# Two graph-attention layers: own queries by rank kept on chip, rank products behind the first query, first loads in the order of their use

## The chip, the cores and the metric

The kernel runs on one core of a Trainium2 chip. The metric is device time in microseconds (us), the median of several runs; smaller is better. The engines are TensorE (PE in the profile, its weight loads PEld), VectorE (DVE), ScalarE (ACT), GpSimd (POOL) and SyncE (SP). SP, ACT and POOL also issue DMA transfers. A line such as L568 is a line of the kernel's file.

## The reference

A graph of N = 2708 nodes has features of width 512. Two layers of the same form are applied, each with its own weights (8 heads of width 64, hidden width 2048):

```python
mask = adj.astype(jnp.float32) + jnp.eye(n, dtype=jnp.float32)
q = (h @ Wq.T + bq).reshape(n, N_HEADS, D_K)
k = (h @ Wk.T + bk).reshape(n, N_HEADS, D_K)
v = (h @ Wv.T + bv).reshape(n, N_HEADS, D_K)
scores = jnp.einsum('nhd,mhd->hnm', q, k) / jnp.sqrt(jnp.float32(D_K))
scores = jnp.where(mask[None, :, :] == 0, jnp.float32(-1000000000.0), scores)
attn = jax.nn.softmax(scores, axis=-1)
ctx = jnp.einsum('hnm,mhd->nhd', attn, v).reshape(n, D_MODEL)
h1 = _layer_norm(h + ctx @ Wo.T + bo, ln1_g, ln1_b)
ff = jax.nn.relu(h1 @ W1.T + b1) @ W2.T + b2
h2 = _layer_norm(h1 + ff, ln2_g, ln2_b)
```

The adjacency is sparse (a node has some nine neighbours with itself), symmetric, given as 2708 x 2708 int32.

## The kernel before, in words

**Lists in place of masks.** `by_edges` turns each row of the adjacency into a list of at most 24 neighbours and then attends only over lists: keys and values are gathered row by row from HBM. A second path, `by_rows`, runs only where a row has too many neighbours; it is not run with these inputs. Nodes are worked on in 22 tiles of 128 (the last, number 21, has 20 nodes). In `first`, tile t means nodes in their given order; everything behind it uses nodes sorted by the length of their list, and tile g then means ranks 128 g to 128 g + 127. `CAPS[g]` is the longest list in tile g, 22 for g = 0 down to 3 for g = 21. The attention goes through the tiles in `order`: 21, 20, then 19, 18, then 8, 9 and so on, two to a block of the feed-forward part.

**Stage 1, `first`.** For each tile, k and v are projected from x (columns of xT, loaded in blocks `xg` of 256 nodes) and written to `kv_d`. At the same time `lists` loads rows of the adjacency (`aj`, two buffers), POOL adds the diagonal (L656), ScalarE squares into `code` (L660), and VectorE takes the greatest eight of each of 11 pieces and merges them (L663 to L670). When all lists are there, `counted` works out the lengths and prefix counts on VectorE (L684 to L732), `ranked` multiplies them with a triangle and with ones on TensorE (L742, L749) to get each node's rank, writes each node's list to its rank in `rec_d` by 22 indirect DMAs (L768), reads all back into `new`, and makes `ident_i`, the node of each rank (L794). `listed` makes `idx` and `minus` of it.

**Stage 2, `first_queries`.** q of all nodes is projected tile by tile in their given order and written to `q_d`, two tiles per DMA (`written`). The attention needs q by rank, and so a gather from `q_d` once all of it is there. To begin earlier, `own_rows` gathers rows of x by rank, `turned_own` transposes them, and `own_query` projects them: at t = 9 (OWN) for tiles 21 and 20, whose q stays on chip in `own`; at t = 11 for tiles 19 and 18, whose q is written to `q_own` in HBM and read back by `asked`. Between these q, `advance` and `through` move the attention on: a generator, `attend`, whose step k multiplies one pair of gathered neighbours with q (`weights`, L991 and L997), weighs the values of the step before (`weigh`, L1010 to L1030), sums the tile that ended two steps before (`sums`) and divides the one that ended three before (`divided`, L1061, making `cx`). `advance` adds to a credit that steps use up; it stops while two finished tiles wait in `got`. `loads` gathers keys and values ahead, into five buffers.

**Stage 3, the blocks.** `attended` transposes cx (L1100), projects with Wo (L568, `o`), adds x by rank and normalises; `turned` transposes the result to `hT`. `feed_forward` runs 16 steps f: pf = W1 times hT (L1265, three PSUM buffers), relu on ScalarE to `ft` (L1273), and, three steps behind, the second product into `a` (L1253). At f = 10 the next block's cx is transposed, at f = 11 its `o` is made, behind f = 15 its `hT`. Keys and values of the next layer are made from each finished block (`keys_values`).

**What sets the order.** On PE, ACT and SP the order of instructions is that of the program text throughout (`manual_schedule`). On POOL this holds in stages 1 and 2, on VectorE in stage 2; elsewhere a scheduler orders these two. A wait at the head of an engine holds whatever is written behind it. So what `advance` writes between two relus stands between them on ScalarE.

Of the kernel before, what the change touches and what calls it, by code (L numbers as in the profile page):

```python
# [18 lines left out]
P = 128  # L19
# [26 lines left out]
OWN = 9  # L46
# [424 lines left out]
def by_edges(ctx: ExitStack, tc: tile.TileContext, x, xT, adj, layers, out, good):  # L471
# [32 lines left out]
    own = {}  # L504
    at = None
# [15 lines left out]
    q_own = dram.tile([N, DM], F32, name="q_own")  # L521
# [280 lines left out]
    def first(w, meanwhile):  # L802
# [20 lines left out]
        load()  # L823
        wk = matrix(w, "Wk", "wk")
        turning = turned_row(cols[1], "bk", 1.0)
# [5 lines left out]
        for t in range(NT):  # L831
            r = size(t)
            xs = tokens(t, 0)
            kv = wts.tile([P, 2 * DM], F32, tag=f"w2_{5 + t % 3}", name="kvs")
            k = project(xs, r, wk, "k")
            if t == 0:
                finish(turning)
            nc.vector.tensor_tensor(kv[:r, :DM], k[:r], bk[:r], ALU.add)
            if t == NT - 1:
                ranked(*counts)  # L840
            v = project(xs, r, wv, "v", other=True)
            nc.scalar.copy(kv[:r, DM:], v[:r])
            if before:
                nc.scalar.dma_start(**before)
            before = dict(out=kv_d[0][t * P : t * P + r, :], in_=kv[:r])
            if t == 0:
                load()
            while done < min(NT, 1 + LEAD * t):
                lists(done)
                done += 1  # L850
                if done == NT:
                    counts = counted()
            meanwhile(t)
            if t == QT:
                wq = matrix(w, "Wq", "wq")
                turning = turned_row(cols[0], "bq", DK**-0.5)
                bq = next(turning)
                finish(turning)
        nc.scalar.dma_start(**before)
        return bq, wq, listed, pa, tokens  # L860

    def first_queries(bq, wq, listed, pa, tokens, meanwhile):

        nonlocal at
        xrs = [own_rows(g) for g in blocks[0]]
# [12 lines left out]
        for t in range(NT):  # L878
# [10 lines left out]
            if t == OWN - 1:  # L889
# [15 lines left out]
        while made:  # L905
            written()

# [11 lines left out]
    def own_query(g, zT, to, bq, wq):  # L919
# [4 lines left out]
        if g in blocks[1]:  # L924
            nc.sync.dma_start(out=q_own[g * P : g * P + r, :], in_=to[:r])
# [183 lines left out]
    class Layer:  # L1109
# [27 lines left out]
        def load_second(self, part, temp):  # L1137
# [3 lines left out]
            def sum_of(one, tag, other):  # L1141
                t, u = row(w, one, tag), temp()
                nc.sync.dma_start(out=u, in_=other.to_broadcast([P, DM]))
                nc.vector.tensor_tensor(t, t, u, ALU.add)
# [200 lines left out]
    def attend(n, got):  # L1345
# [15 lines left out]
        for k, step in enumerate(steps):  # L1361
            if step:
                g, s0, c, i, last = step
                if i == 0:
                    t = Tile(g, q)
# [3 lines left out]
                if i == 1 and g != order[-1]:  # L1369
# [36 lines left out]
    early = {}  # L1406

    def beside_keys(t):
# [3 lines left out]
        if t > NT - 3:  # L1412
            now.load_second(t + 2 - NT, temp)
# [3 lines left out]
    def beside_queries(t):  # L1417

        if len(now.w2) < 5:
            now.load_w1(len(now.w1), nc.scalar)  # L1420
            now.load_w2(len(now.w2), nc.scalar)
        if t > OWN:
            advance(1.0 if t < NT - 7 else 0.45)
        if t == NT - 7:
# [3 lines left out]
        if t == NT - 6:  # L1428
# [10 lines left out]
    for j in range(len(now.w1), NFC // 2):  # L1439
        now.load_w1(j)  # L1440
        now.load_w2(j)
    behind, pool = None, []
    for n in range(NL):
# [26 lines left out]
        turning = projecting = None  # L1470
        for k, block in enumerate(blocks):
# [4 lines left out]
            for f, zs in enumerate(now.feed_forward(block, hs, hT)):  # L1476
# [8 lines left out]
                if more and f == 10:  # L1485
# [29 lines left out]
                if not last and not more:  # L1515
# [7 lines left out]
                    if f == 7:  # L1523
                        finish(ahead)
                        pool += nxt.preloaded(order[:8], temp)
            if not last:
# [79 lines left out]
```

## Time and profile before

| | |
|---|---|
| median of 3 runs | 1984.96 us (1980.67 to 1987.98) |
| profiled execution | 1984.12 us, of which span 1982.0 us |
| TensorE busy | 1903.5 us, 96% of the span; granted clock 0.985 |
| VectorE, ScalarE, POOL busy | 1303.1, 934.6, 798.3 us |
| DMA | 367.96 MB, 186 GB/s over the span |
| stage 1 | to about 172 us; adjacency, x and weights come at about 330 GB/s |
| stage 2 | 172 to 285 us |
| first feed-forward block | 290 to about 357 us |

All times of the trace count from the span's start. In a timeline each line is: start, length, engine, line, operation, written tile <- read tiles, shape, count, and in brackets how long the engine was idle before it and what ended that. A matmul of 128x512 in float32 counts as two records in it. SPq and ACTq are the issuing of DMAs by these engines.

### The profile page before, as it was taken

How to read it: one execution, taken by the hardware profiler on the slowest of the kernel's cores; microseconds unless marked ns; L12 is line 12 of the kernel's file. 1: busy time of each engine (PE TensorE's matmuls, PEld its weight loads, DVE VectorE, ACT ScalarE, POOL GpSimd, SP SyncE). 2: the span in 40 equal slices, each digit the busy share in tenths (PEclk: the TensorE clock that was granted, in tenths of full speed). 3: DMA queues.
4: the chain of work that ended last, by engine and by line, in shares of the span. 5: the costliest groups of instructions: out<-in, count | busy, mean ns of one | idle time of the engine just before them, and what ended most of it. 6: DMA issues, size and time to landing. Idle time of an engine off the chain costs nothing. (4 is left out here: it accounts for less than half of the span.)

```text
span 1982.0 us, 20873 instructions
## 1 busy us (share of the span) xinstructions
PE 1903.5 (96%) x6162; PEld 1104.5 (56%) x6162; DVE 1303.1 (66%) x2140; ACT 934.6 (47%) x3219; POOL 798.3 (40%) x708
## 2 busy tenths in 40 slices
PE   8999888999999999999999997999999999999997
PEld 3443344565656556566566643556666566666664
DVE  6884478675957969568442025888587989777421
ACT  4660235464545646447441112665446765655320
POOL 3104436362634636435210023455356655544210
PEclk9999899999999999999999998999999999999998
DMA  8988658464745747455310746756465766554100
GB/s 321 357 296 293 191 200 296 154 208 143 227 154 174 236 150 246 154 173 176 133 58 22 225 157 225 258 182 212 155 208 186 244 205 225 177 188 151 42 11 13
DMA packets 131518, 367.96 MB, mean 186 GB/s; under 512 B 16701, under 2 KB 36525, under 8 KB 128687
## 3 DMA queue, kind: packets, MB, share of 16 engines
q0 software_dynamic: 69104, 246.35, 37.6%
q1 hardware_dynamic: 55780, 103.86, 15.3%
q10 hardware_dynamic: 6510, 16.34, 2.2%
q8 instruction: 50, 0.82, 0.2%
q14 instruction: 74, 0.60, 0.1%
HBM read 315.14 MB, written 51.35 MB: 185 GB/s over the span
## 5 line engine op out<-in xcount | busy, mean ns | idle before, releaser
L952 POOL DMA_INDIRECT kv<-kv_d,idx x420 | 547.0, 1302 | 494.0 <-DVE acc L1030 337.2
L1253 PE MATMUL a<-w,ft 128*128 128x512 f32 (+1 forms) x1408 | 665.3, 597 | 9.5 <-ACT ft L1273 9.5
L1265 PE MATMUL pf<-hT,w 128*128 128x256 f32 (+1 forms) x2816 | 638.2, 374 | 15.8 <-ACT ft L1273 8.0
L1265 PEld LDWEIGHTS pf<-hT,w 128*128 128x128 f32 x2816 | 523.2, 192 | 193.4 <-issue 107.7
L1253 PEld LDWEIGHTS a<-w,ft 128*128 128x128 f32 (+1 forms) x1408 | 255.9, 186 | 234.1 <-issue 198.3
L1273 ACT ACTIVATE ft<-pf,b 128x256 f32<-128x256 f32 (+1 forms) x352 | 157.9, 458 | 424.4 <-PE pf L1265 424.1
L991 DVE TENSOR_TENSOR kv<-kv,q 128x1024 f32<-128x1024 f32 (+3 forms) x222 | 256.5, 1158 | 144.6 <-DMA kv<-kv_d,idx 122.0
L1017 ACT ACTIVATE kv<-kv,p 128x64 f32<-128x64 f32 x1232 | 311.0, 335 | 5.0
L997 DVE TENSOR_REDUCE sc<-kv 128x16 f32<-128x1024 f32 (+3 forms) x222 | 254.6, 1153 | 1.0
L1030 DVE TENSOR_TENSOR acc<-acc,kv 128x1024 f32<-128x1024 f32 (+2 forms) x178 | 203.8, 1145 | 35.9 <-ACT kv L1017 35.4
L1090 POOL TENSOR_TENSOR rd<-va,mhalf 128x1 f32<-128x1 f32 (+1 forms) x88 | 85.7, 974 | 270.0 <-DVE va L1088 268.6
L1010 ACT ACTIVATE p<-sc,minus 128x8 f32<-128x8 f32 (+1 forms) x420 | 103.3, 295 | 190.3 <-DVE sc L997 189.9
L1023 DVE TENSOR_TENSOR kv<-kv,p 128x512 f32<-128x512 f32 (+1 forms) x178 | 121.5, 683 | 69.5 <-ACT p L1010 69.5
L568 PE MATMUL o<-wo,cT 128*128 128x512 f32 (+1 forms) x352 | 155.1, 593 | 0.5 <-ACT cT L1105 0.5
L568 PEld LDWEIGHTS o<-wo,cT 128*128 128x128 f32 (+1 forms) x352 | 65.1, 186 | 86.5 <-issue 75.8
L1061 ACT ACTIVATE cx<-acc,su 128x64 f32<-128x64 f32 (+1 forms) x352 | 88.5, 333 | 42.4 <-DVE su L1053 34.9
L1285 DVE TENSOR_TENSOR h<-a,h 128x512 f32<-128x512 f32 (+1 forms) x44 | 29.7, 677 | 106.0 <-PE a L1253 105.9
L1094 DVE SCALAR_TENSOR_TENSOR h<-h,rd,ln_b 128x512 f32<-128x512 f32 (+1 forms) x88 | 65.8, 748 | 48.1 <-POOL rd L1090 48.1
L660 ACT ACTIVATE code<-aj 128x2708 bf16<-128x2708 int32 (+1 forms) x22 | 73.3, 3330 | 48.1 <-POOL aj L656 41.2
L663 DVE MAX8 tops<-code 128x8 f32<-128x247 f32 (+2 forms) x242 | 82.8, 400 | 18.6 <-ACT code L660 18.5
L1017 ACT ACTIVATE acc<-kv,p 128x64 f32<-128x64 f32 (+1 forms) x352 | 88.8, 334 | 1.4
L568 PE MATMUL k<-wk,xg 128*128 128x512 f32 (+1 forms) x176 | 82.1, 611 | 6.8 <-DMA wk<-in_Wk 6.7
(132 smaller groups left out, 1466.3 us busy)
## 6 DMA issues: line engine op xcount, KB each, us to landing
aj<-in_adj SPq DMA_DIRECT2D x21, 1354.0 KB, 11.8
w<-in_W SPq DMA_DIRECT2D x26, 512.0 KB, 4.8
kv_d<-kvs ACTq DMA_DIRECT2D x21, 512.0 KB, 7.2
xg<-in_xT SPq DMA_DIRECT2D x20, 512.0 KB, 7.0
kv<-kv_d,idx POOLq DMA_INDIRECT x420, 5.6
q_d<-qs SPq DMA_DIRECT2D x22, 256.0 KB, 4.7
zT_d<-zT SPq DMA_DIRECT2D x22, 256.0 KB, 5.3
xb_d<-h SPq DMA_DIRECT2D x21, 256.0 KB, 5.3
```

The source lines that it names most:

```text
L568: nc.tensor.matmul(o[:r], xs(c), wm[:, c, :], start=(c == 0), stop=(c == NC - 1))
L952: nc.gpsimd.indirect_dma_start(out=to, out_offset=None, in_=table[:, :], in_offset=bass.IndirectOffsetOnAxis(ap=s, axis=0), bounds_check=N ...
L991: nc.vector.tensor_tensor(kv[:r, :c, :DM], kv[:r, :c, :DM], self.q[:r].unsqueeze(1).to_broadcast([r, c, DM]), ALU.mult,)
L997: nc.vector.tensor_reduce(self.sc[:r, s0 : s0 + c, :], kv[:r, :c, :DM].rearrange("p s (h d) -> p s h d", d=DK), AX.X, ALU.add,)
L1010: nc.scalar.activation(p[:r, s, :], self.sc[:r, s, :], AF.Exp, bias=minus[:r, g, s : s + 1])
L1017: nc.scalar.activation(to[:, i, hd], kv[:r, i, DM + h * DK : DM + (h + 1) * DK], AF.Copy, scale=p[:r, s0 + i, h : h + 1],)
L1023: nc.vector.tensor_tensor(to[:, 0, :].rearrange("p (h d) -> p h d", d=DK), kv[:r, 0, DM:].rearrange("p (h d) -> p h d", d=DK), p[:r, s0, : ...
L1030: nc.vector.tensor_tensor(self.acc[:r, :c, :], self.acc[:r, :c, :], kv[:r, :c, DM:], ALU.add)
L1061: nc.scalar.activation(cx[:r, hd], self.acc[:r, 0, hd], AF.Copy, scale=self.su[:r, h : h + 1])
L1253: nc.tensor.matmul(a[:r], fts[f][:, c0 : c0 + r], self.w2[f // 2][:, f % 2, :], start=(f == 0), stop=(f == NFC - 1),)
L1265: nc.tensor.matmul(pf[:, :w], self.w1[f // 2][:, c, f % 2 * P : f % 2 * P + P], hT[:, c, :w], start=(c == 0), stop=(c == NC - 1),)
L1273: nc.scalar.activation(ft[:, :w], pf[:, :w], AF.Relu, bias=self.b1[:, f : f + 1])
```

## The change

1. First loads: the first block of x is loaded in two halves. SP issues the first half, then the first quarter of Wk, bk, the rest of Wk, bq, and then the second half; before, bq and bk came first, then the whole block and Wk.
2. Rank products: `ranked` moves from between k and v of the last key tile to behind the first q of stage 2; the rows of x by rank are gathered right behind it.
3. Own queries: three tiles (21, 20, 19) in place of four. All three are gathered and transposed together at t = 11, and their q stays on chip; `q_own` is gone. Tile 18's q comes from `q_d` like all later ones: `asked` gives None until all q are written, and `attend` then yields None, at which `advance` stops.
4. The attention beside the queries is paced anew: `through(0)` and the first block's transpositions at t = 16 in place of 15, its `o` at t = 17 in place of 16, 0.6 in place of 0.45 credit behind that.
5. The two sums of bias rows with b2 and bo (`load_second`) are made behind q 3 in place of in stage 1.
6. The last three pairs of W1 and W2 pieces are loaded on ACT's queue at f = 0, 2, 4 of the first block, in place of SP's queue before it.
7. In the first block, the next block's transpositions and `o` come at f = 11 and 12 in place of 10 and 11. In layer 0's blocks POOL keeps the order of the program text.

```diff
-OWN = 9
+OWN = 11
@@ first
-            nc.sync.dma_start(out=t[:, :, :bw], in_=chunked(xT)[:, :, b : b + bw])
             xg.append(t)
+            step = bw if i else P
+            for a in range(0, bw, step):
+                nc.sync.dma_start(
+                    out=t[:, :, a : a + step], in_=chunked(xT)[:, :, b + a : b + a + step]
+                )
+                yield
...
-        cols = given_column(w, "bq"), given_column(w, "bk")
-        load()
-        wk = matrix(w, "Wk", "wk")
-        turning = turned_row(cols[1], "bk", 1.0)
+        wk = wts.tile([P, NC, DM], F32, tag="wk", name="wk")
+        halves = load()
+        next(halves)
+        for c in range(NC):
+            nc.sync.dma_start(out=wk[:, c, :], in_=chunked(w["Wk"])[:, c, :])
+            if c == 0:
+                cols = [given_column(w, "bk")]
+        cols.append(given_column(w, "bq"))
+        finish(halves)
+        turning = turned_row(cols[0], "bk", 1.0)
...
-            if t == NT - 1:
-                ranked(*counts)
@@ first_queries
-        xrs = [own_rows(g) for g in blocks[0]]
...
             q = project(tokens(t, 1), r, wq, "q", other=t % 2 > 0)
+            if t == 0:
+                ranked(*counts)
+                xrs = [own_rows(g) for g in order[:3]]
...
-                for g in blocks[0]:
+                for g in order[:3]:
                     own[g] = at.tile([P, DM], F32, tag="q", name="q", bufs=QB)
...
-            if t in (OWN, OWN + 2):
-                k = (t - OWN) // 2
-                zTs = [turned_own(g, xr) for g, xr in zip(blocks[k], xrs)]
-                for g, xr, zT in zip(blocks[k], xrs, zTs):
-                    own_query(g, zT, to.get(g, xr), bq, wq)
+            if t == OWN:
+                zTs = [turned_own(g, xr) for g, xr in zip(order, xrs)]
+                for g, zT in zip(blocks[0], zTs):
+                    own_query(g, zT, to[g], bq, wq)
                     advance(0.5)
-                xrs = [own_rows(g) for g in blocks[1]] if k == 0 else []
+            if t == OWN + 2:
+                own_query(order[2], zTs[2], to[order[2]], bq, wq)
             meanwhile(t)
         while made:
             written()
+        all_made.append(True)
@@ own_query
-        if g in blocks[1]:
-            nc.sync.dma_start(out=q_own[g * P : g * P + r, :], in_=to[:r])
@@ asked
+        if n == 0 and not all_made:
+            return None
         q = at.tile([P, DM], F32, tag="q", name="q", bufs=QB)
-        if n == 0 and g not in blocks[1]:
-            gather(q[:r], q_d[0], ident_i[:r, g : g + 1])
-        else:
-            table = q_own if n == 0 else q_d[n]
-            nc.sync.dma_start(out=q[:r], in_=table[g * P : g * P + r, :])
+        fetch(n, q, q_d[n], g)
@@ attend
                 if i == 0:
-                    t = Tile(g, q)
+                    while q is None:
+                        q = asked(n, g)
+                        if q is None:
+                            yield None
+                    t, q = Tile(g, q), None
...
-                if i == 1 and g != order[-1]:
+                if i > 0 and q is None and g != order[-1]:
@@ beside_keys, beside_queries
-            now.load_second(t + 2 - NT, temp)
+            now.load_second(t + 2 - NT, temp, sums)
...
+        if t == 3:
+            for total, other in sums:
+                nc.vector.tensor_tensor(total, total, other, ALU.add)
...
-            advance(1.0 if t < NT - 7 else 0.45)
-        if t == NT - 7:
+            advance(1.0 if t < NT - 6 else 0.6)
+        if t == NT - 6:
             through(0)
...
-        if t == NT - 6:
+        if t == NT - 5:
@@ by_edges, the blocks
-    for j in range(len(now.w1), NFC // 2):
-        now.load_w1(j)
-        now.load_w2(j)
...
+        in_order = ExitStack()
+        if n == 0:
+            in_order.enter_context(tc.manual_schedule(engines={mybir.EngineType.Pool}))
...
-                if more and f == 10:
+                if more and f == 10 + (k + n == 0):
...
-                if more and f == 11:
+                if more and f == 11 + (k + n == 0):
...
-                advance(PACE[n] if k else 1.1 if f < 10 else 0.4)
+                advance(PACE[n] if k else 1.1 if f < 11 else 0.4)
...
+                if k == 0 and len(now.w1) < NFC // 2 and f % 2 == 0:
+                    now.load_w1(len(now.w1), nc.scalar)
+                    now.load_w2(len(now.w2), nc.scalar)
```

More of the change, by code (lines that the diff above doesn't have):

```diff
@@ L504, in by_edges @@
     own = {}
+    all_made = []
     at = None
@@ L520, in by_edges @@
     q_d = [dram.tile([N, DM], F32, name=f"q_d{n}") for n in range(NL)]
-    q_own = dram.tile([N, DM], F32, name="q_own")
     zT_d = [None] + [dram.tile([NT, P, NC, P], F32, name=f"zT_d{n}") for n in range(1, NL)]
@@ L817, in tokens @@
             if c0 == 0 and len(xg) < 2 * XBS:
-                load()
+                finish(load())
             xs = xg[i + again * XBS]
             return lambda c: xs[:, c, c0 : c0 + size(t)]
-        cols = given_column(w, "bq"), given_column(w, "bk")
-        load()
-        wk = matrix(w, "Wk", "wk")
-        turning = turned_row(cols[1], "bk", 1.0)
+        wk = wts.tile([P, NC, DM], F32, tag="wk", name="wk")
[8 more added lines that the diff above has]
+        turning = turned_row(cols[0], "bk", 1.0)
         bk = next(turning)
@@ L846, in first @@
             if t == 0:
-                load()
+                finish(load())
             while done < min(NT, 1 + LEAD * t):
@@ L855, in first @@
                 wq = matrix(w, "Wq", "wq")
-                turning = turned_row(cols[0], "bq", DK**-0.5)
+                turning = turned_row(cols[1], "bq", DK**-0.5)
                 bq = next(turning)
@@ L859, in first, with first_queries @@
         nc.scalar.dma_start(**before)
-        return bq, wq, listed, pa, tokens
-    def first_queries(bq, wq, listed, pa, tokens, meanwhile):
+        return bq, wq, counts, ranked, listed, pa, tokens
+    def first_queries(bq, wq, counts, ranked, listed, pa, tokens, meanwhile):
         nonlocal at
-        xrs = [own_rows(g) for g in blocks[0]]
         made = []
@@ L1135, in load_w2, with load_second @@
             self.w2.append(t)
-        def load_second(self, part, temp):
+        def load_second(self, part, temp, later=None):
             w = self.w
@@ L1143, in sum_of @@
                 nc.sync.dma_start(out=u, in_=other.to_broadcast([P, DM]))
-                nc.vector.tensor_tensor(t, t, u, ALU.add)
+                if later is None:
+                    nc.vector.tensor_tensor(t, t, u, ALU.add)
+                else:
+                    later.append((t, u))
                 return t
@@ L1405, in by_edges @@
     ahead = attend(0, got)
-    early = {}
+    early, sums = {}, []
     def beside_keys(t):
@@ L1525, in by_edges @@
                         pool += nxt.preloaded(order[:8], temp)
+            in_order.close()
             if not last:
```

## The prediction

> **What bounds the kernel now.** I began with the busy times of the page: TensorE is busy for 96% of the span, so only its idle time and its slow clock can be won, and each matmul taken away counts in full.
>
> ```profile
> PE 1903.5 (96%) x6162; PEld 1104.5 (56%) x6162; DVE 1303.1 (66%) x2140; ACT 934.6 (47%) x3219; POOL 798.3 (40%) x708
> ```
>
> Next I cut the first 360 us, the part that the diff touches, where TensorE stops (busy time by stretch; the columns are the stretch, its length, busy us and instructions of PE, PEld, DVE, ACT and POOL, granted clock, DMA share, GB/s).
>
> ```profile
> 6.72:159.64 152.92, 152.86 (x360) 67.23 (x360) 122.03 (x438) 82.90 (x43) 19.55 (x55) 1.00 0.93 333
> 159.64:172.16 12.52, 8.06 (x17) 3.30 (x17) 8.12 (x27) 0.00 (x0) 1.11 (x1) 0.73 0.68 236
> 206.76:217.69 10.93, 1.59 (x8) 1.21 (x8) 1.41 (x4) 0.23 (x1) 7.10 (x8) 0.66 0.52 152
> 285.16:290.37 5.21, 0.00 (x0) 0.00 (x1) 5.17 (x8) 3.47 (x16) 2.29 (x2) 0.86 0.81 297
> 308.36:323.00 14.64, 7.81 (x24) 4.08 (x25) 14.11 (x18) 8.51 (x33) 9.19 (x8) 0.88 1.01 366
> ```
>
> There are five stalls: the start (6.72 us), the rank matmuls (from 159.64), the rows of x by rank (206.76), the turned rows of the first block (285.16), and the middle of the first feed-forward block (308.36). Each one also lowers the clock after it. The timeline of TensorE shows what each waits for:
>
> ```profile
> 164.10 1.22 PE L742 MATMUL pr<-hot,tri 128*128 128x264 f32 x2 [4.46 <-DVE kvs L838]
> ...
> 213.55 0.58 PE L1100 MATMUL tp<-ident,xr 20*128 20x20 f32 x4 [6.79 <-DMA xr<-in_x,ident_i]
> 216.68 1.09 PE L1100 MATMUL tp<-ident,xr 128*128 128x128 f32 x4 [2.55 <-DMA xr<-in_x,ident_i]
> 217.69 8.66 PE L568 MATMUL q<-wq,zT 128*20 128x512 f32 x16
> ...
> 290.37 6.88 PE L1265 MATMUL pf<-hT,w 128*128 128x148 f32 x32 [5.21 <-ACT hT L1105]
> ...
> 313.20 2.34 PE L1265 MATMUL pf<-hT,w 128*128 128x148 f32 x8 [4.84 <-ACT ft L1273]
> ...
> 319.88 1.27 PE L1265 MATMUL pf<-hT,w 128*128 128x148 f32 x8 [1.99 <-ACT ft L1273]
> ```
>
> The last two are not ScalarE's own slowness. Its relus stand in order behind attention weights, these behind VectorE, and VectorE behind a gather of q (timelines of POOL, DVE and ACT):
>
> ```profile
> 299.71 2.46 POOL L952 DMA_INDIRECT q<-q_d,ident_i  x1 [0.30 <-issue]
> ...
> 307.34 1.22 DVE L991 TENSOR_TENSOR kv<-kv,q 128x1024 f32<-128x1024 f32 x1 [5.93 <-issue]
> ...
> 317.54 2.02 ACT L1061 ACTIVATE cx<-acc,su 128x64 f32<-128x64 f32 x8
> ```
>
> From 350 us on, the waits of TensorE are small (10.6 us up to 1180), and the change leaves that part as it is.
>
> [...] 16 passes of 128x512 take 8.66 us at 217.69, where 32 warm ones at 241.31 take 13.90, so a long stop costs 1.7 us more. A wait of 1.99 us costs nothing here, one of 2.80 (at 1650 us) some 1.8. [...] So a gather from q_d waits for all twelve writes; the trace has it after the last one. [...] the stretch from 308 shows a DMA share of 1.01.
>
> **The change, part by part.** Times are those of the profiled execution (span 1982.0 us, 1984.12 in all; the median is 1984.96, 0.84 above). From the first block's end on, the written order of all engines is unchanged, so the sum ends there.
>
> *First loads.* The first real load is issued at 0.79 in place of 1.72 us, and the first matmul needs 512 KB in place of 768: an estimate of 1.4 us earlier. This does not reach the end whole. The last key tiles wait for VectorE to empty PSUM (0.88 us at 156), and VectorE works through lists that come through two adjacency buffers: 7 us from issue to landing at the end of that stage, 0.5 on POOL, 3.3 on ScalarE, in a loop. Ahead of the first adjacency load lie as many bytes as before, so that loop starts 0.9 us earlier. I take 0.9 (bounds 0 and 1.4). One more issue on SP costs 0.45 us of SP alone, hidden by the transfers.
>
> *Rank matmuls behind the first q.* They wait for VectorE's counting, to 163.9. TensorE now does the last v (3.4) and, once PSUM is free at 163.9, the first q (3.4), then the four rank products warm (1.8), to 169.1; eleven more q at 3.43 end at 206.9. Before, ten q were done at 206.76; now twelve are: +6.9 us. The ranks themselves hardly move: VectorE's wait for a bias row (2.37 us at 168.11) goes, the q ahead of the rank products takes its place: 0.3 us earlier. So **the wait for x by rank stays**, and I count nothing for it. The two bias sums move behind q 3, where VectorE idles 2.7 us a q.
>
> *Three q in one group.* The third transposition waits for a third gather, issued at 211.9 (where the first kv gather was); with the second's 6.1 us it lands at 217.9. The first own q starts at 218.2: -0.5. The kv gathers behind it on POOL start 1.3 us later; their first reader comes at 223.5, so that is covered. The fourth own q (3.43 us) and its transposition (0.5) are gone: +3.9. Two writes and two reads of q_own leave SP, and with them VectorE's wait of 6.85 us at 268.
>
> *Attention beside the q.* Own q end at 226.7, q 12, 13, own 19 and q 14 to 16 at 247.3. Next come the transpositions of cx. VectorE's list up to the sum of tile 20, at 0.6 us per 512 elements, ends at 248.3, ScalarE's cx 2 us later: TensorE waits 2.7 us there (new), and with even odds loses 1.9 of clock: 3.7 together. Then q 17, both o, q 18 to 21 and the transpositions take 25.8: 276.4 after the 0.9 from the start. ScalarE no longer has tile 18's weights ahead of hT, so hT takes 1.4 in place of 5.2 us. Feed-forward begins at **277.7 in place of 290.37**.
>
> *The q of tile 18.* It now comes from q_d, so it waits for the last q. From that q's end on VectorE (276.1), the write takes 3, POOL 1, the gather 4.5 to 5: 285. (Before, 294.88 to 307.34, 12.5 us, with POOL busy and the DMA engines full.) Two steps of attention are written behind the first relu, so relu 1 stands behind tile 18's first weights. From 285: four VectorE passes of 1.13 us, of which three come before the weights (288.5), weights 2.5, two loads issued 1.1, relu: 292.5. TensorE has run out at 284 and waits 8.6 us. Then ScalarE alone sets the pace: four more weights at 2.5, one at 0.3, two cx at 2.0, four load issues (2.2), four relus: relu 5 at 310.7. Before, the same point was 319.9, since only the three steps of tile 8 (12.2 us) stood behind the late q. **Gain at that point: 9.1 us.** The wait of 2.8 us ahead of it costs up to 1.7 of clock: -0.8. Attention's projection one f later leaves h no slack (h was done 3 us before its transposition): -0.5.
>
> *POOL by hand, W loads on ScalarE.* POOL's order behind the first block is the old one: nothing. The last six W loads no longer come in one burst at 295 to 301; they are needed from f = 10 on, some 20 us after issue, and took 8.2 us on that queue.
>
> Sum: 9.1 - 0.8 - 0.5 = 7.8, about **8 us**: 1984.96 - 8 = 1977.
>
> **Rivals.** (1) *Short waits.* cx is ready sooner (no clock loss, 1 us less wait: 3 us), q lands at 283 (2 us), the start brings 1.4: 13 to 15 us, 1971. For it: fewer transfers at 276 to 290 than in the burst before. Against: q can't overtake the last write.
> (2) *Another wait in the same place.* VectorE's order puts the next layer's bias column (L1161 before) ahead of tile 18's products. If this column takes the 15.2 us that its neighbour took, VectorE starts at 292.7 and the gain is about 0: 1985. Against: that was under a full DMA load; other columns took 6.5 to 7.2.
> (3) *Slower.* The block ends 24 us of ScalarE work after q 18 is there. Break-even is q landing at 294, a loss of 10 us at 304, 28 us after the last q. That needs POOL's two kv gathers ahead of the q gather to be held by a buffer that VectorE frees late: 1995. Against: their buffers are free from 262 on.
>
> **How the numbers follow.** About 0.5% (10 us) is what a measurement of this kernel can tell from no change. Forecast 0.56 (4 to 12 us of gain), rival 1 0.26, rival 2 0.12, rival 3 0.06. Faster: rival 1 and the forecast's upper end (0.11), 0.37; slower 0.06; same 0.57. The range from 1967 to 1986 takes in rival 1 and most of rival 2; the forecast's own is 1973 to 1981.
>
> **What would show it.** Right: TensorE's first matmul near 5.3 us; no stop of over 1 us at the rank products; a stop from about 206 to 218; feed-forward from about 278; then a stop of 7 to 9 us behind ScalarE's relu, with VectorE waiting for q. Wrong: no stop at f = 4, feed-forward after 283, or stops beyond 360 us that were not there.

## The result and the profile after

| | before | changed kernel |
|---|---|---|
| median | 1982.49 us (1976.43 to 1987.98, 12 runs) | 1979.45 us (1975.20 to 1986.72, 12 runs) |
| ratio to before | | 0.9981, 95% interval 0.9968 to 0.9994 |
| once more, with the experiments | 1982.02 us (42 runs) | 1978.20 us (21 runs); 0.9977, 0.9970 to 0.9985 |
| profiled execution: span | 1982.0 us | 1978.1 us |

The gain is 3 to 4.5 us. It is clear of noise, since both intervals lie below 1, but it is under the 0.5% of the prediction's cases, and about half of the 8 us forecast or less.

The page's busy times say where a gain can't have come from: TensorE has only 2.4 us less work, the fourth own query and its transposition less what a slower clock adds (granted 0.983 over the span, before 0.985).

```profile
PE 1901.1 (96%) x6150; PEld 1100.9 (56%) x6150; DVE 1300.5 (66%) x2139; ACT 933.6 (47%) x3218; POOL 790.7 (40%) x708
```

The timeline of TensorE in the changed kernel answers to the stops shown of before:

```profile
4.77 5.21 PE L568 MATMUL k<-wk,xg 128*128 128x512 f32 x8 [4.77 <-DMA wk<-in_Wk]
...
161.93 3.70 PE L568 MATMUL q<-wq,xg 128*128 128x512 f32 x8 [0.93 <-DVE kvs L849]
...
211.78 0.58 PE L1108 MATMUL tp<-ident,xr 20*128 20x20 f32 x4 [6.61 <-DMA xr<-in_x,ident_i]
214.61 1.09 PE L1108 MATMUL tp<-ident,xr 128*128 128x128 f32 x4 [2.25 <-DMA xr<-in_x,ident_i]
216.33 1.09 PE L1108 MATMUL tp<-ident,xr 128*128 128x128 f32 x4 [0.63 <-DMA xr<-in_x,ident_i]
217.35 8.29 PE L568 MATMUL q<-wq,zT 128*20 128x512 f32 x16
...
277.66 4.31 PE L1276 MATMUL pf<-hT,w 128*128 128x148 f32 x32 [0.54 <-ACT hT L1113]
...
290.45 2.34 PE L1276 MATMUL pf<-hT,w 128*128 128x148 f32 x8 [6.45 <-ACT ft L1284]
...
307.19 1.36 PE L1276 MATMUL pf<-hT,w 128*128 128x148 f32 x8 [2.43 <-ACT ft L1284]
...
384.32 6.58 PE L568 MATMUL v<-wv,zT 128*128 128x512 f32 x8 [5.56 <-DVE kvs L1327]
```

Read from the top. The start is earlier, the stop of 4.46 us ahead of the rank products has become 0.93 us ahead of the first q, the stop for x by rank is still there, the 5.21 us ahead of the feed-forward part are 0.54, and the stop ahead of f = 4, which waits for the relu of f = 1, is there as expected. (The first relu, of f = 0, is done by 279.4 us. Some texts of the experiments call the one of f = 1 "the first relu".) The last line is the surprise. It lies at 384 us, well behind the first block, in a part that the prediction took as unchanged: the value projection of layer 1's keys and values (`keys_values`) stands still for 5.56 us, and then runs its eight records in 6.58 us in place of some 3.6: the granted clock is 0.56 in this stretch, where it was 1.00 in the projection before the stop. Before, the same matmul waited 0.27 us and took 3.70:

```profile
390.10 3.70 PE L568 MATMUL v<-wv,zT 128*128 128x512 f32 x8 [0.27 <-DVE kvs L1316]
```

Both traces have the same 2816 records of `pf` in the same order. So the start of one and the same record in both timelines, before minus after, is the gain up to that point:

| record of `pf` | before, us | after, us | gain |
|---|---|---|---|
| first (block 1, f = 0) | 290.4 | 277.7 | 12.7 |
| 65th (block 1, f = 8) | 319.9 | 307.2 | 12.7 |
| 129th (block 2, f = 0) | 358.3 | 347.2 | 11.1 |
| 193rd (block 2, f = 8) | 397.1 | 394.2 | 2.9 |
| 257th (block 3, f = 0) | 439.0 | 435.9 | 3.1 |
| last | 1961.5 | 1957.7 | 3.8 |

11.1 us are won by the end of the first block, 8.2 of them are lost between 378 and 391 us, and behind that the number moves by some 2 us (2.9 to 5.1). The question is what the 8.2 us were lost to. This table is used for every experiment below, because it shows where a gain comes and goes, which a median with an interval 3 to 8 us wide can't. But it is one execution of each kernel. A second execution of the changed kernel (the last experiment) has a gain of 12.4 us at the 129th record, 6.4 at the 257th and 8.6 at the end: 1.3, 3.3 and 4.8 more than the first. So places and waits are read from it, and differences of a few us at the end are not.

### The profile page after: what moved, and what is told of

The parts are those of the page before. It is cut to its first block, busy times and chain, and to the rows that moved or that the text cites. A ratio compares the mean times of both kernels' runs of the same rounds, so it can differ in the third digit from the quotient of the medians.

```text
span 1978.1 us, 20841 instructions
## 1 busy us (share of the span) xinstructions
PE 1901.1 (96%) x6150; PEld 1100.9 (56%) x6150; DVE 1300.5 (66%) x2139; ACT 933.6 (47%) x3218; POOL 790.7 (40%) x708
## 5 line engine op out<-in xcount | busy, mean ns | idle before, releaser
L1335 POOL DMA_INDIRECT kv_d<-kvs,ident_i x22 | 23.3, 1060 | 164.2 <-ACT kvs L1329 97.1
```

## The experiments

Each ratio is to the kernel before, run beside it. "Gain" means the table's column, from the experiment's profiled execution.

### Two parts alone: first loads, rank products

The kernel before with part 1 of the change alone:

```diff
-        load()
-        wk = matrix(w, "Wk", "wk")
+        halves = load()
+        next(halves)
+        for c in range(NC):
+            nc.sync.dma_start(out=wk[:, c, :], in_=chunked(w["Wk"])[:, c, :])
...
+        finish(halves)
```

> The kernel before with one part of the change: the first loads in the order of their use, with half of x's first block. The prediction gave this part 1.4 us at the first matmul, of which 0.9 us was to reach the end; the trace of the changed kernel shows 1.95 us at the first matmul and 3.2 us from the second tile on. If TensorE carries it through the first 210 us: 3 us at the end, 1979.5 to 1980.5 us. If the first own query still waits for x by rank, which follows GpSimd's and VectorE's ranks and not TensorE, and the gathers set what follows: 0 to 1 us, 1982 to 1983 us.

1982.24 us; ratio 0.9992 (0.9982 to 1.0002). TensorE starts 1.86 us earlier and carries that unchanged to the last q at 280 us, through the wait for x by rank, so the second theory is wrong on the place, though its time is the one that came. At the start of block 2 0.9 us is left. By the medians this part is worth about 1 us (1983.25 less 1982.24), near what the forecast put down, but its interval takes in no gain at all.

The kernel before with the rank products and the gathers of x behind the first q, and no more:

```diff
-            if t == NT - 1:
-                ranked(*counts)
...
             q = project(tokens(t, 1), r, wq, "q", other=t % 2 > 0)
+            if t == 0:
+                ranked(*counts)
+                xrs = [own_rows(g) for g in blocks[0]]
```

> The kernel before with one part of the change: the rank matmuls and the gathers of x by rank behind the first q, with the first own query still behind the ninth q. TensorE's stop of 6.5 us ahead of the first q goes (the changed kernel shows 8.5 us gained there), but the rows of x by rank come no earlier. If the stop only moves: TensorE waits some 6 to 10 us longer ahead of the first own query, and the time is 1982 to 1984 us. If it is not all paid back there: 1978 to 1981 us.

1983.16 us; ratio 0.9997 (0.9984 to 1.0011): nothing. The timeline of TensorE shows the stop in its new place, 11.55 us where before had 6.79:

```profile
164.95 3.70 PE L568 MATMUL q<-wq,xg 128*128 128x512 f32 x8 [0.93 <-DVE kvs L838]
...
212.88 0.58 PE L1100 MATMUL tp<-ident,xr 20*128 20x20 f32 x4 [11.55 <-DMA xr<-in_x,ident_i]
```

The gain is 5.4 us at the third q and 0.4 us at the own query. Alone the part pays nothing. In the changed kernel OWN = 11 puts two more q into the wait. Parts 3 to 5 of the change were not run alone, so what each brings to the 12.7 us at the first `pf` is not shown.

### The last loads of W1 and W2

The changed kernel with the six last loads on SP in one burst again:

```diff
+    for j in range(len(now.w1), NFC // 2):
+        now.load_w1(j)
+        now.load_w2(j)
...
-                if k == 0 and len(now.w1) < NFC // 2 and f % 2 == 0:
-                    now.load_w1(len(now.w1), nc.scalar)
-                    now.load_w2(len(now.w2), nc.scalar)
```

> The last six loads of W1 and W2 are issued by SyncE in one burst behind the last q again, as in the kernel before; all else as in the changed kernel. The prediction put the burst beside the gather of tile 18's q as a cost of the kernel before, and charged the change 1.1 us of ScalarE for each pair of loads. If the burst is what counts: the q of tile 18 lands 3 to 8 us later than 284.0 us, the first relu at 293 to 298, and the gain at the end of the first block is 4 to 8 us in place of 11.1; 1979 to 1983 us. If ScalarE's issues are what counts: fifth relu up to 4 us earlier, 1975 to 1979 us.

1983.18 us; ratio 1.0003 (0.9993 to 1.0012): without this part the whole change brings nothing. The first theory holds. In the timelines of VectorE the first product with tile 18's q waits for its gather, in the changed kernel and then in this one:

```profile
284.06 2.36 DVE L999 TENSOR_TENSOR kv<-kv,q 128x1024 f32<-128x1024 f32 x2 [0.93 <-DMA q<-q_d,ident_i]
```

```profile
287.70 2.36 DVE L999 TENSOR_TENSOR kv<-kv,q 128x1024 f32<-128x1024 f32 x2 [4.46 <-DMA q<-q_d,ident_i]
```

POOL issues that gather at the same time in both (280.57 and 280.34 us); it lands 3.6 us later beside the burst. The busy times by stretch say why (the last columns are granted clock, DMA share and GB/s), again the changed kernel and then this one:

```profile
280.00:290.00 10.00, 4.00 (x20) 2.17 (x18) 8.04 (x12) 4.19 (x18) 5.44 (x5) 0.89 0.68 200
```

```profile
280.00:290.00 10.00, 4.17 (x22) 2.34 (x20) 4.34 (x7) 1.98 (x8) 4.97 (x5) 0.86 0.98 340
```

A DMA share of 0.98 and 340 GB/s: the DMA engines are full with weights issued at 277.5 to 281.7 us, which nobody needs before f = 10 at 321.5 us. VectorE falls from 8.04 to 4.34 us busy while it waits, TensorE then stops for 9.92 us ahead of f = 4 and 5.05 us ahead of f = 8, and the gain goes from 12.5 us (first record) to 6.8 (65th) and 4.5 (129th). The stop ahead of the values takes the rest (3.99 us of it here).

On the other side of the same edit, the two issues on ScalarE cost it nothing. The timeline of ScalarE in the changed kernel, with ACTq for the issues:

```profile
288.11 0.35 ACT L1025 ACTIVATE acc<-kv,p 128x64 f32<-128x64 f32 x1
288.21 0.37 ACTq L1135 DMA_DIRECT2D w<-in_W  x1
288.36 0.57 ACT L1025 ACTIVATE acc<-kv,p 128x64 f32<-128x64 f32 x2
288.76 0.39 ACTq L1142 DMA_DIRECT2D w<-in_W  x1
288.84 1.29 ACT L1025 ACTIVATE acc<-kv,p 128x64 f32<-128x64 f32 x5
290.03 0.36 ACT L1284 ACTIVATE ft<-pf,b 128x148 f32<-128x148 f32 x1
```

The eight passes run from 288.11 to 290.13, 2.02 us, exactly as long as eight passes with no issue between them (2.02 at 290.81). The relu of f = 1 follows at once. The other two pairs lie among eight passes each too, which take 2.02 us at 295.42 and 2.01 at 304.85.

### POOL's order

The list of the change says that POOL keeps the order of the program in layer 0's blocks. In the code that ends with the first block (`in_order.close()` stands behind its last step), so only this block has it.

Three theories for the lost 8.2 us. (1) POOL in the order of the program sends a gather of keys and values late, and attention falls behind. (2) Taking the contexts at f = 11 and 12 holds attention back. (3) Attention, bound by its gathers, can't follow a TensorE that is 11 us earlier; whatever is done, a stop appears.

POOL free in the first block:

```diff
-            in_order.enter_context(tc.manual_schedule(engines={mybir.EngineType.Pool}))
+            pass
```

> POOL is no longer put in the order of the program in layer 0's blocks; all else as in the changed kernel (about 1979.5 us; the kernel before about 1982.5). Theory 1, POOL's order costs attention its lead: the gather 9.3 goes out ahead of the two short powers again, some 10 us earlier than at 340.6 us, the gathers behind it follow, VectorE adds bk to the keys of layer 1 about 5 us earlier, TensorE's 5.56 us before the values of layer 1 shrink to under 1 us, and the time is 1972 to 1975. Theory 3, attention can't follow TensorE whatever POOL's order: 9.3 may go out earlier, but the stop before the values stays at 4 to 6 us and the time within 1.5 us of 1979.5.

1975.73 us (8 runs); ratio 0.9963 (0.9949 to 0.9978). The gain is 10.6 us at the 65th record, 8.5 at the 129th, 8.9 at the 257th: the stop ahead of the values is gone. The time lies between the ranges of the two theories. The gather called 9.3 brings tile 9's fourth pair of neighbours, in two DMAs. In the timeline of POOL both stand in the changed kernel behind the second of two short powers of the norm (`rd`), which itself waits for VectorE:

```profile
338.82 1.60 POOL L1098 TENSOR_TENSOR rd<-va,mhalf 128x1 f32<-128x1 f32 x1 [2.43 <-DVE va L1096]
340.60 1.52 POOL L962 DMA_INDIRECT kv<-kv_d,idx  x1 [0.19 <-issue]
342.42 1.46 POOL L962 DMA_INDIRECT kv<-kv_d,idx  x1 [0.30 <-DVE kv L999]
```

With POOL free the first of the two stands ahead of both powers and the second between them, each 6.2 us earlier:

```profile
334.35 0.99 POOL L962 DMA_INDIRECT kv<-kv_d,idx  x1 [0.30 <-issue]
335.36 0.65 POOL L1098 TENSOR_TENSOR rd<-va,mhalf 128x1 f32<-128x1 f32 x1
336.19 1.56 POOL L962 DMA_INDIRECT kv<-kv_d,idx  x1 [0.18 <-issue]
```

What hangs on it is seen on VectorE. First the changed kernel, where it waits for that gather at 344 us, for a next one at 365 us, and so comes to the keys of layer 1 at 383.60; then POOL free, where the first of these waits is missing:

```profile
348.33 1.23 DVE L999 TENSOR_TENSOR kv<-kv,q 128x1024 f32<-128x1024 f32 x1 [4.19 <-DMA kv<-kv_d,idx]
...
371.68 1.22 DVE L999 TENSOR_TENSOR kv<-kv,q 128x1024 f32<-128x1024 f32 x1 [6.81 <-DMA kv<-kv_d,idx]
...
383.60 1.27 DVE L1327 TENSOR_TENSOR kvs<-k,bk 20x512 f32<-20x512 f32 x2
```

```profile
367.98 1.22 DVE L999 TENSOR_TENSOR kv<-kv,q 128x1024 f32<-128x1024 f32 x1 [4.64 <-DMA kv<-kv_d,idx]
...
380.64 1.43 DVE L1327 TENSOR_TENSOR kvs<-k,bk 20x512 f32<-20x512 f32 x2
```

L1327 takes k out of PSUM. The four projections of a pair of tiles (k, v, k, v) share a PSUM tag of three buffers, so the fourth can't start before the first k is out. In the kernel before this began at 389.38 us, so VectorE is only 5.8 us earlier in the changed kernel where TensorE was 11.1 us earlier.

But the earlier gather is only a part of why the stop is gone. With POOL free VectorE comes to the keys 3.0 us earlier (380.64 against 383.60), and TensorE comes to the projection before the stop 2.6 us later (377.64 against 375.06). The two together make up the 5.56 us. So theory 1 is shown for the late gather and for some 3 us of the stop. An estimate from these numbers is that a TensorE as early as in the changed kernel would still have stopped for some 2.6 us.

TensorE's delay is the price of a free POOL. The gather of tile 18's q is issued at 282.82 us in place of 280.57 (why is not shown), TensorE stops for 8.59 us in place of 6.45 ahead of f = 4, and the gain at the 65th record is 10.6 us in place of 12.7. The scheduler also puts a product of attention ahead of the norm of the next block's h, and TensorE waits 1.87 us for that h at 343.84. This is no price of the free POOL: the second execution of the changed kernel waits 1.77 us for it too, and from the 65th to the 129th record it loses 2.0 us, the free POOL 2.1.

To keep the one and not the other, POOL's order by hand was ended at f = 8:

```diff
+                if (n, k, f) == (0, 0, 8):
+                    in_order.close()
```

> POOL's order by hand ends at feed-forward step 8 of the first block, in place of its last step; all else as in the changed kernel. Theory 1 (POOL's order at the end of the first block sends the gather 9.3 out behind two short powers): 9.3 goes out at about 336 us as with the free POOL, but the first relu stays at 290 us where the free POOL had it at 292.7; no stop over 2 us before the values, the gain stays at 9 to 11 us, 1970 to 1975 us. If what helped with the free POOL was its order near 275 us (a gather of keys ahead of those of the queries), the stop of 4 to 6 us stays, 1978 to 1981 us.

1975.57 us (7 runs); ratio 0.9949 (0.9930 to 0.9968). The gather goes out early again (335.23 and 337.07 us), the stop ahead of the values is gone, and the gain doesn't fall there (5.9 us at the 129th record, 7.0 at the 257th). But the 9 to 11 us expected were not seen: this execution is late already in the key tiles of stage 1 (the first transposition of x by rank comes at 214.96 us, 3.2 us later than in the changed kernel), and it waits 2.25 us for h and then takes 7.22 us for twelve records of `a` that take 5.53 in the changed kernel. So TensorE comes to the keys 5.2 us later than in the changed kernel (380.21) and VectorE only 1.1 us earlier (382.46). This trace therefore doesn't tell whether the early gather alone would have removed the stop.

### The contexts one step earlier

```diff
-                if more and f == 10 + (k + n == 0):
+                if more and f == 10:
...
-                if more and f == 11 + (k + n == 0):
+                if more and f == 11:
...
-                advance(PACE[n] if k else 1.1 if f < 11 else 0.4)
+                advance(PACE[n] if k else 1.1 if f < 10 else 0.4)
```

> The short queries and the turned contexts are taken at feed-forward steps 10 and 11 of the first block again, not one step later; all else as in the changed kernel. Theory 2, that shift costs attention its lead: the stop of 5.56 us before the values of layer 1 goes, and the time is 1972 to 1975. Theories 1 and 3: the stop stays at 4 to 7 us, and the time is between 1978.5 and 1983 (TensorE may wait 1 to 3 us more at step 10, for contexts that are not ready).

1975.95 us (7 runs); ratio 0.9959 (0.9945 to 0.9973). In its profiled execution (1979.09 us) theory 2 fails: a stop of 3.97 us, 6.47 us for the eight records of the values behind it, and the changed kernel's gains of 11.4 us at the 129th record and 3.1 at the 257th. Yet the median is 2 to 3.5 us below that of the changed kernel. The execution that was traced is the second slowest of the seven, five of which took 1973.79 to 1976.10 us. Whether these had the stop is not known, and this is left open.

### Keys and values later

In block 2 the keys and values of layer 1 are made at f = 7 and 8:

```diff
+                late = 2 * (k + n == 1 and n == 0)
-                if f in (5, 6) and behind:
+                if f in (5 + late, 6 + late) and behind:
```

> The keys and values of layer 1 for the first block are made two feed-forward steps later in the second block (steps 7 and 8 in place of 5 and 6); all else as in the changed kernel. Theory 3, attention and with it VectorE's evacuation of the keys is late by about 6 us there, and TensorE only stops because the values want PSUM at that point: the stop of 5.56 us and the slow clock behind it go, and the time is 1971 to 1975. Theory 1 expects the same sign but that attention, still 5 us late, stops TensorE at its next taking of contexts: 1975 to 1979. That the stop is made up for later anyway: within 1 us of 1979.5.

1975.95 us (5 runs); ratio 0.9955 (0.9937 to 0.9972). The stop ahead of the values shrinks to 1.44 us. But the gain still falls, from 13.8 us at the 129th record to 8.9 at the 257th: TensorE now waits 1.87 and 1.17 us for relus at 423 to 426 us. The first of these relus stands on ScalarE behind the division of cx, for which ScalarE has waited 6.30 us for VectorE (420.80). So here late attention does stop TensorE, by way of ScalarE's order. The stop is partly moved, not removed.

Both edits together, POOL free and keys later:

> Both the free POOL and the later keys (steps 7 and 8) in one kernel. If either theory alone is right, the second edit adds nothing to the better of the two, 1971 to 1975. If each takes a part of the 8.2 us that are given back between 378 and 391 us, this one is the fastest, 1969 to 1972.

1979.44 us (21 runs); ratio 0.9981 (0.9972 to 0.9989): no better than the changed kernel. It has the costs of both. The gain falls to 6.8 us at the 129th record, where TensorE waits 2.07 us for h and then takes 7.21 us for the twelve records of `a`, and to 3.1 at the 257th by the same two stops for relus as above (1.87 and 1.17 us), although there is no stop at the values. So the reading that each edit takes a part of the 8.2 us is wrong.

### VectorE taken out of the keys

This sets theory 3 apart: POOL's order and the late gather stay, but TensorE's way out no longer leads through VectorE's queue.

```diff
-                nc.vector.tensor_tensor(kv[:r, :DM], k[:r], self.bk[:r], ALU.add)
+                nc.scalar.copy(kv[:r, :DM], k[:r])
@@ project, for these two tiles
+        nc.tensor.matmul(o[:r], ones[0:1, :r], row[0:1, :], start=False, stop=True)
```

> In the first block's keys for layer 1 (two tiles), bk is added by one more 1-row matmul each (about 2 x 0.45 us on TensorE) and ScalarE, not VectorE, takes the sum out of PSUM; all else as in the changed kernel. If VectorE's queue, behind attention steps that wait for gathers, is what stops TensorE before the values of layer 1 (5.56 us there, and about 2.9 us of slow clock with it): no stop over 1 us there, a gain over the kernel before of 9 to 11 us behind that point in place of 2.9, and 1971 to 1975 us. If attention itself can't follow TensorE (theory 3 in its strong form), the stop comes back at the next taking of contexts, between 398 and 440 us, and the time is 1978 to 1981.

1975.02 us (8 runs); ratio 0.9952 (0.9936 to 0.9968). Its lines lie three further down in the file. The gather 9.3 is as late as in the changed kernel (issued at 339.56), and VectorE waits for gathers at the same places:

```profile
347.15 1.22 DVE L1002 TENSOR_TENSOR kv<-kv,q 128x1024 f32<-128x1024 f32 x1 [4.06 <-DMA kv<-kv_d,idx]
369.12 1.23 DVE L1002 TENSOR_TENSOR kv<-kv,q 128x1024 f32<-128x1024 f32 x1 [5.42 <-DMA kv<-kv_d,idx]
```

TensorE comes to the last k at the same time as in the changed kernel (375.06 us there), and goes on:

```profile
375.08 3.70 PE L569 MATMUL k<-wk,zT 128*128 128x512 f32 x8
379.76 3.70 PE L569 MATMUL v<-wv,zT 128*128 128x512 f32 x8
```

The gain is 12.1 us at the 129th record and 10.5 at the 257th, and 12.1 at the end. There is no stop later that takes it back. Theory 3 in its strong form is wrong for this kernel: attention is late, and TensorE's waits behind that point come to no more than in the other kernels. What stopped it was VectorE's place in the evacuation of k.

The control, the same edit in the kernel before:

> The kernel before, with ScalarE in place of VectorE taking the first block's keys for layer 1 out of PSUM (bk added by a 1-row matmul), as in the experiment that keeps the gain there. If the stop ahead of the values is made by TensorE being early, the kernel before, with 0.27 us of it, has nothing to win: 1982 to 1984.5 us. If taking VectorE out of these projections is worth 4 us by itself: 1977.5 to 1980 us.

1983.93 us; ratio 1.0010 (1.0000 to 1.0021). The edit by itself wins nothing. The medians differ by 1.9 us, the wrong way, and the interval reaches from no cost to 4 us. In the trace the extra matmul costs 1.06 us each, more than the 0.45 expected, which is one of a projection's eight records (3.60 us), where the extra matmul has two (from the start of k to that of v it takes 4.50 us at 379.15, where before takes 3.44, and this twice; gain -1.4 us at the 257th record). So it is the change that makes the stop that the edit removes.

Together with the contexts one step earlier:

> The changed kernel with ScalarE taking the first block's keys for layer 1 out of PSUM, and the turned contexts taken at feed-forward steps 10 and 11 again. If both edits only remove the one stop ahead of the values: as the first alone, 1974 to 1976 us. If the second, which alone was 3.5 us faster than the changed kernel though its profile still has 3.97 us of that stop, brings something of its own: 1970 to 1973 us.

1973.76 us (6 runs); ratio 0.9957 (0.9941 to 0.9972), against 0.9952 for the edit alone. The time lies between the two ranges expected, and by the intervals the second edit adds nothing to the first. Its trace loses 6.4 us between the 129th record (15.6) and the 257th (9.2), of which 2.84 are a stop at 353.43 us, for VectorE to empty `a`, that the first edit alone doesn't have. Either version beats both kernels, by some 8 us against before (the kernel before beside them ran at 1983.25 and 1982.02) and 3 to 6 against the changed kernel.

### The changed kernel once more

> The changed kernel itself, once more, beside the other kernels of this call. If the stop ahead of the values of layer 1 is a fixed consequence of the order: a stop of 4 to 7 us there again, and 1978.5 to 1980.5 us. If it comes and goes with the landing of single gathers from one execution to the next: a stop that differs by more than 2 us from 5.56, with the span differing by about as much.

1978.20 us (21 runs). The profiled execution, with a span of 1973.3 us, has the stop again, 4.59 us, with the same gather issued at 339.26 us and the same waits of VectorE. So both traced executions have the stop, and it doesn't come and go with single gathers. (The median is 0.3 us below the range expected.) What differs between the two lies in part elsewhere: 1.4 us already at the first `pf`, the eight records behind the stop, which took 5.40 us here and 6.58 in the first profile, and some 1.5 us behind the start of block 3. An execution with the stop can thus be as fast as one without it (span 1973.3 us here, 1973.7 with POOL free).

```profile
382.01 5.40 PE L568 MATMUL v<-wv,zT 128*128 128x512 f32 x8 [4.59 <-DVE kvs L1327]
```

## Why the prediction was right or wrong

The time came out 2.5 us above the forecast and inside its own range, but with luck. First, the forecast started from 1984.96 us, the median of three runs, and over twelve the kernel before stands at 1982.49. So the gain is 5 us off (3.0 where 8 was forecast, below the forecast's own 4 to 12 us; 3.8 when measured again), and half of that doesn't show in the time. Second, two errors of opposite sign stand in the sum. By its own steps:

**First loads.** 1.4 us at the first matmul, 0.9 passed on. Measured 1.95 us at the first matmul in the changed kernel. For the part alone it was 1.86, with 0.9 left at the start of block 2 and about 1.0 by the medians, not clear of noise. Right in size as far as this can be told.

**Rank products.** Twelve q done at 206.9 us: they end at 205.18 (167.25 + 37.93). That the wait for x by rank stays, and the part alone is worth nothing, was shown by its experiment (11.55 in place of 6.79 us).

**Three q, attention beside them.** Own q from 218.2: 217.35. The new wait for cx was put at 2.7 us and, at even odds, half of 1.9 of clock: 3.7 together. The timeline has 1.68 us of wait, and then a q of 5.29 us where the one before it takes 3.60: 3.37 together, a shorter wait and the whole loss of clock. Feed-forward from 277.7: 277.66. So close a hit is luck: own q were 0.9 us early, and 247.3 + 3.7 + 25.8 - 0.9 makes 275.9, not the 276.4 that the sum goes on with.

**The q of tile 18.** 285: 284.06. Of its parts, the write with its landing took 3.7 us (the last of the twelve writes is issued at 276.9 us, and POOL, idle for 8.08 us, issues the gather at 280.57) where 3 was put, and the gather 3.5 from issue to landing where POOL's 1 and 4.5 to 5 were. That it gains from the burst being gone was said only in passing; the experiment shows that the burst takes 3.6 us at this point and 5 to 6 us by f = 8, which is as much as the whole change brings. The late bias column (rival 2) didn't come about: VectorE waited 0.41 us for it at 281.09.

**ScalarE's chain.** Here a term was mis-sized. The relu of f = 1 was to be done at 292.5 us and TensorE's stop to be 8.6 us: measured 290.4 and 6.45. TensorE was to go on at 310.7, behind the relu of f = 5; it did at 307.19. The sum charged 1.1 us of ScalarE for each pair of load issues, 3.3 us for three pairs. They overlap ScalarE's arithmetic and cost 0 (eight passes with two issues among them take 2.02 us, as without). That is nearly all of the difference between the 9.1 us of gain forecast at this point and 12.7 measured. The rest about cancels: q came 0.9 us early and the passes took a little less than put down, but ScalarE waited 0.90 and 0.80 us for VectorE, which the sum had at nothing.

**Clock and h.** -0.8 and -0.5: the gain fell from 12.7 to 11.1, so -1.6.

**The end of the sum.** "From the first block's end on, the written order of all engines is unchanged, so the sum ends there." This is the step that failed. The order is unchanged in the program's text (VectorE's own order there is the scheduler's, and a few of its products stand elsewhere), but the engines reach that point with other leads: TensorE 11.1 us earlier, VectorE 5.8. A wait of 0.27 us before told that there was no slack between the two. Of the same kind is "POOL's order behind the first block is the old one: nothing": true behind the block, but POOL's order inside it is new, and at 340 us it puts a gather behind a power that waits for VectorE. How much of VectorE's lateness that makes is shown only in part (3.0 us with POOL free). The price of the stop is 8.2 us in one profiled execution (5.56 of stop, and 2.88 in the eight records behind it, 6.58 less 3.70) and 6.0 in the other. By the medians the kernel that takes only VectorE out of the keys stands 3.2 to 4.4 us below the changed kernel (1975.02 us against 1978.20 and 1979.45). The medians don't follow the stop everywhere: with POOL free and the keys later there is none, at 1979.44 us, and with the contexts one step earlier there is one, at 1975.95. The prediction did name "stops beyond 360 us that were not there" as what would show it wrong, and there was one.

Sum against sum: 7.8 forecast, +3.3 for the issues, -8.2 for the stop, makes 2.9, which is the gain that the table shows at 394 us.

## What to carry to other kernels

Follow a gain past the end of the part that was edited, up to the next place where two engines meet: a wait of a few tenths there (0.27 us before), between an engine that becomes earlier and one that becomes less so (11.1 and 5.8 us), was a stop of 5.56 us in the changed kernel. Where one engine must not stop, don't let its buffers be freed by an engine whose queue also waits for transfers; the same work on another queue removed the stop here, at a cost of two small matmuls of 1.06 us each. And bulk loads that nobody needs yet are worth moving away from a single short gather that everything waits for: beside the burst it landed 3.6 us later, and without that part this change brought nothing (1983.18 us, ratio 1.0003).

## What the runs showed of the hardware that was not expected

DMAs issued by ScalarE in the middle of its work did not delay it: eight passes with two issues between them took 2.02, 2.02 and 2.01 us at three places, as eight without (2.02).

Behind a stretch of transpositions and short waits TensorE ran slower. From 246.17 to 249.87 us in the changed kernel, 3.7 us, TensorE does only the eight transpositions of cx and waits 1.68 and 0.15 us, and the next q takes 5.29 us, at a granted clock of 0.68:

```profile
246.17 0.42 PE L1108 MATMUL tp<-ident,cx 20*128 20x20 f32 x4
248.27 0.33 PE L1108 MATMUL tp<-ident,cx 128*128 128x128 f32 x1 [1.68 <-ACT cx L1069]
...
249.87 5.29 PE L568 MATMUL q<-wq,xg 128*128 128x512 f32 x8
```

So the forecast's reading of the kernel before, that a wait of 1.99 us costs nothing, doesn't carry over to this place. In ten profiled executions of kernels with this stretch, nine had the slow q (5.18 to 5.30 us), and one, that with the burst of loads, ran it in 3.60 us behind a stretch as long (3.69 us). In the four profiled kernels that don't wait for cx there, from 0.85 to 2.11 us pass from the first of these transpositions to the next q, and it took 3.60 to 3.67 us. At the transpositions of the next block's h, a wait of 1.87 us (POOL free) or 1.77 (the changed kernel's second execution) was followed by twelve records of `a` in 5.53 us, as where the changed kernel's first execution doesn't wait, and a wait of 2.07 (POOL free and keys later) or 2.25 us (POOL's order ended at f = 8) by 7.21 and 7.22. What makes the one slow and the other not is shown by no run here.
